# A graph network kernel: a third x1 buffer, own buffers for the ninth slot, transposed sums, and the diagonal taken off TensorE

## The chip, the cores and the metric

The kernel runs on one NeuronCore of a Trainium2 chip. Its time is the device time in microseconds of one execution; the figure compared is the median of several executions. The engines are TensorE (PE for its matmuls and PEld for its weight loads in the profile), VectorE (DVE), ScalarE (ACT) and GpSimd (POOL). Each works through its own queue in order, so an instruction that waits holds back all that stand behind it on its engine. DMA transfers are issued from the queue of SyncE (SP).

## The reference

There are 32 independent batch elements, each a graph of N = 512 nodes with D = 128 features. The adjacency matrix has about one entry in sixteen set, and a full diagonal.

```python
# layer 0
a = adj + eye(N); d = a.sum(axis=2) ** -0.5          # 0 where the degree is 0
x = layernorm(x + (d[:, :, None] * a * d[:, None, :]) @ (x @ w0) + b0)
# layer 1
m_j, m_i = x @ W1[:D], x @ W1[D:]
pre = m_j[:, None, :, :] + m_i[:, :, None, :] + b1     # [B, i, j, D]
msg = gelu(layernorm(pre) * g1 + be1)                  # exact gelu
agg = einsum('bijo,bij->bio', msg, adj)
upd = layernorm(concat([x, agg]) @ W2 + b2) * g2 + be2
out = layernorm(x + upd)
```

The costly part is layer 1: a layer norm and a gelu for each edge (i, j).

## The kernel before

The nodes of an element are cut into C = 4 chunks of P = 128. An adjacency matrix is thus 4 x 4 blocks (q, c). For each row of each block the kernel lists its edges, works through them one edge per row at a time, and leaves zeros of the matrix alone.

**Slots.** Eight *list slots* hold the eight first edges of each row in each block. A small *ninth slot* (`EXTRA`) holds one more edge per row of the four diagonal blocks. Two *shared slots* hold what is left over, packed. The list slots and the shared slots take four turns each (one for each q), the ninth slot one, so an element takes 8 x 4 + 1 + 2 x 4 = 41 turns of the main loop. In the ninth slot `gathered` loads a vector of 516 numbers to all partitions and `gathers` compares it with the partition's number (`s`, 128 x 516); in the other slots both have 2052 numbers. `gathers` also starts a transposing DMA of `s` into `mt`.

**One turn.** `pairs` (TensorE) gathers, by one-hot matmuls, the pre-activation of 512 edges into a PSUM tile `u` (three buffers). One turn later `sums` (DVE, L733) adds the part of the node itself and writes `u_sb`, and `weights` (POOL, L748) makes `sw`, the one-hot matrix times the adjacency values. Two turns later `messages` (ACT, L762) writes the gelu `m` in four activations. Three turns later `aggregate` (TensorE, L771) adds `sw` times `m` into the PSUM tile `agg`. The shared slots skip `sums`; there ACT reads `u` itself. `raw` of a slot is loaded five turns ahead of it, and its `s` is made three turns ahead.

**Work beside the turns.** The other steps are generators that are advanced a few steps per turn. `prepare` runs a plan of six of them, each given a stretch of turns: `layer0` (26 steps) from turn 41 before its element begins to turn 19 before, then `lists`, `parts`, `factors`, `more` and `shared`. Counted in the turns of element b, `layer0(b+2)` occupies turns 41 to 62. After the last `aggregate` of an element, at turn 43, `finish(b)` is appended to `todo` and advanced one step per turn, ahead of the plan's steps of that turn. `finish` transposes `agg`, multiplies by W2, adds the bias, normalises (L194 and L196 on DVE, L199 to L205 on POOL, L208 on ACT), applies g2 and be2 and adds x1 (L642, L644, L646, on POOL), normalises again and stores the result.

For the turns from 43 on this gives, on the engines of the change:

- ACT, turn 43: copy of agg (L780), m, and layer 0's copies; turn 44: m, `aggt` (L629) and copies; turn 47: m, four counts (L291), four scaled copies that make `s` (L295); turn 49: m, the activation `un`; turn 52: m(50), the activation that writes `x1` of element b+2; then m(51), m(52) and, at turn 55, the activation `o_sb`.
- DVE, turn 51: u_sb(50), `y` (L311) and its statistics; turn 52: u_sb(51) and steps of `shared`; turn 53: u_sb(52), the statistics of `un`.
- POOL, turn 50 to 52: one of L642, L644 and L646 each, behind that turn's `sw`; the small steps of y's layer norm stand in turn 51, those of `un`'s in turn 54.

The order of ACT, POOL and DVE is the order in which the program is written (`manual_schedule`). The order on TensorE and SP is chosen by the framework, which also places the semaphores: a tile with `bufs=n` has n buffers for its tag, and a write into a buffer waits until the readers of the tile that held it before are done.

In layer 0 the diagonal of `adj + eye` is not added to the matrix: the node's own part is one more matmul, of the identity with `s` (L306), into the same PSUM sum.

Of the kernel before, what the change touches and what calls it, by code (L numbers as in the profile page):

```python
# [8 lines left out]
F32 = mybir.dt.float32  # L9
BF16 = mybir.dt.bfloat16  # L10
I32 = mybir.dt.int32
U32 = mybir.dt.uint32
AF = mybir.ActivationFunctionType
ALU = mybir.AluOpType
# [4 lines left out]
P = 128  # L19
# [4 lines left out]
PAD = 4  # L24
# [3 lines left out]
def bcast(ap, n):  # L28

    return ap.unsqueeze(1).to_broadcast([ap.shape[0], n, ap.shape[-1]])  # L30
# [16 lines left out]
def sparse_path(ctx, tc, x, adj, w0, b0, w1, b1, g1, be1, w2, b2, g2, be2, out, most):  # L47
# [21 lines left out]
    nc = tc.nc  # L69
    B, N, D = x.shape  # L70
    C = N // P
# [3 lines left out]
    node = ctx.enter_context(tc.tile_pool(name="node", bufs=1))  # L75
    small = ctx.enter_context(tc.tile_pool(name="small", bufs=2))
    onehot = ctx.enter_context(tc.tile_pool(name="onehot", bufs=2))
# [3 lines left out]
    ps_g = ctx.enter_context(tc.tile_pool(name="ps_g", bufs=1, space=PSUM))  # L81
# [3 lines left out]
    ident = const.tile([P, P], F32, name="ident")  # L85
# [45 lines left out]
    node_p = const.tile([P, 1], F32, name="node_p")  # L131
# [12 lines left out]
    for name, src in (("b0", b0), ("b1", b1), ("g1", g1), ("be1", be1), ("b2", b2), ("g2", g2), ("be2", be2)):  # L144
        t = const.tile([P, D], F32, name=f"{name}_row")
# [34 lines left out]
    for k in range(n_sd):  # L180
        t = const.tile([P, C, C, P], BF16, name=f"sd_rows{k}")
# [31 lines left out]
    def bank(key):  # L213
        return ps.tile([P, 512], F32, tag="ps", name=key)

    def transposed(src, key):

        pt = bank(f"pt_{key}")
        for c in range(C):
            nc.tensor.transpose(pt[:, c * P : (c + 1) * P], src[:, c, :], ident)  # L220
        return pt
# [3 lines left out]
    def pause(n):  # L225

        for _ in range(n):
            yield

    def layer0(b):  # L230

        st = state[b] = {}
# [6 lines left out]
        a_t = big.tile([P, C, C, WIDE], F32, tag="a_t", name=f"a_t_{b}", bufs=2)  # L239
# [6 lines left out]
        for mc in range(C):  # L246
            pt = bank(f"pa_{b}_{mc}")
# [4 lines left out]
            if mc == 2:  # L252
                psup = bank(f"psup_{b}")
# [29 lines left out]
        rsqrt(rdeg, degp)  # L283
        dinv = small.tile([P, C], F32, tag="dinv", name=f"dinv_{b}")
        nc.gpsimd.tensor_sub(dinv, rdeg, none)
        xb = node.tile([P, C, D], F32, tag="t2", name=f"xb_{b}")
        nc.gpsimd.tensor_tensor(xb, xs, bcast(rows["b0"], C), ALU.add)

# [4 lines left out]
        s = node.tile([P, C, D], F32, tag="t1", name=f"s_{b}")  # L293
        for c in range(C):
            nc.scalar.activation(  # L295
                s[:, c, :], psup[:, c * P : (c + 1) * P], AF.Copy, scale=dinv[:, c : c + 1]
            )
        yield from pause(2)
        pt = bank(f"pconv_{b}")
        for c in range(C):  # L300
            o = pt[:, c * P : (c + 1) * P]
            for mc in range(C):
                nc.tensor.matmul(
                    o, a_t[:, mc, c, :P], s[:, mc, :], start=(mc == 0), stop=False
                )
            nc.tensor.matmul(o, ident, s[:, c, :], start=False, stop=True)  # L306
            if c % 2:
                yield
        y = node.tile([P, C, D], F32, tag="t3", name=f"y_{b}")
        for c in range(C):  # L310
            nc.vector.scalar_tensor_tensor(  # L311
                y[:, c, :], pt[:, c * P : (c + 1) * P], dinv[:, c : c + 1], xb[:, c, :], ALU.mult, ALU.add
            )
        x1 = node.tile([P, C, D], F32, tag="x1", name=f"x1_{b}", bufs=2)
        yield from layernorm(y, x1, f"l0_{b}")
        st["x1"] = x1
        yield
        pt = transposed(x1, f"x1_{b}")
# [32 lines left out]
        for q in range(C + 1):  # L351
# [4 lines left out]
            if q < C:  # L356
                pt = bank(f"pv_{b}_{q}")
# [96 lines left out]
    def shared(b):  # L454

        st = state[b]
# [22 lines left out]
        pt = bank(f"po_{b}")  # L479
# [32 lines left out]
        pt = None  # L512
        for k in range(len(chunks) + 1):
            if k:
                nc.vector.tensor_scalar(sj_f[:, chunks[k - 1]], pt, node_p, None, ALU.is_equal)  # L515
            if k < len(chunks):
                pt = bank(f"pj_{b}_{k}")
# [6 lines left out]
        for n in range(C * C + 1):  # L524
            if n:
                nc.scalar.copy(sent[:, n - 1], pt[:, : SHARED * WIDE].rearrange("p (k w) -> p k w", w=WIDE))  # L526
            if n < C * C:
                pt = bank(f"pl_{b}_{n}")
                for k in range(SHARED):
# [4 lines left out]
                        start=True,  # L534
                        stop=True,
# [28 lines left out]
        n_i = SHARED * C + 1  # L564
        pt = bank(f"pidx_s_{b}")
# [5 lines left out]
        nc.gpsimd.tensor_scalar(ve[:, :n_r], picked[:, 1, :], 0.0, None, ALU.max)  # L571
        nc.gpsimd.tensor_scalar(ve[:, n_r:], var[:, own, 0], 0.0, None, ALU.max)
        yield
        idx_r = node.tile([n_i, N], BF16, tag="idx_rs", name=f"idx_rs_{b}")
        nc.scalar.copy(idx_r, pt[:n_i, :])
        sd = small.tile([P, n_r + C], F32, tag="sd_s", name=f"sd_s_{b}", bufs=1)
        nc.scalar.activation(sd, ve, AF.Sqrt, bias=eps_t, scale=1.0 / D)
# [6 lines left out]
        pt = bank(f"psd_s_{b}")  # L584
# [38 lines left out]
    def finish(b):  # L623

        st = state.pop(b)
        pt = transposed(st["agg_sb"], f"g_{b}")
        yield
        aggt = node.tile([P, N], F32, tag="f1", name=f"aggt_{b}")
        nc.scalar.copy(aggt, pt)  # L629
        yield  # L630
        pt = bank(f"pu_{b}")
        for c in range(C):
            o, here = pt[:, c * P : (c + 1) * P], slice(c * P, (c + 1) * P)
            nc.tensor.matmul(o, st["x1t"][:, here], w2_sb[:, 0, :], start=True, stop=False)
            nc.tensor.matmul(o, aggt[:, here], w2_sb[:, 1, :], start=False, stop=True)
        yield
        u = node.tile([P, C, D], F32, tag="f0", name=f"u_{b}")
        nc.vector.tensor_tensor(u, pt.rearrange("p (c d) -> p c d", d=D), bcast(rows["b2"], C), ALU.add)
        yield
        un = node.tile([P, C, D], F32, tag="f1", name=f"un_{b}")  # L640
        yield from layernorm(u, un, f"l1_{b}")
        nc.gpsimd.tensor_tensor(un, un, bcast(rows["g2"], C), ALU.mult)  # L642
        yield
        nc.gpsimd.tensor_tensor(un, un, bcast(rows["be2"], C), ALU.add)  # L644
        yield
        nc.gpsimd.tensor_tensor(un, un, st["x1"], ALU.add)  # L646
        yield
        o_sb = node.tile([P, C, D], F32, tag="o_sb", name=f"o_sb_{b}")
        yield from layernorm(un, o_sb, f"l2_{b}")
        yield  # L650
        nc.sync.dma_start(out[b].rearrange("(c p) d -> p c d", p=P), o_sb)
# [4 lines left out]
    EXTRA = SLOTS  # L656
# [5 lines left out]

    def gathered(b, t):

        raw = onehot.tile([P, 3, (C * N + PAD) // 3 + 2], BF16, tag="raw", name=f"raw_{b}_{t}", bufs=1)
        if t < SLOTS:
            src, n0, n = state[b]["idx_d"], t * C, C
        elif t == EXTRA:
            src, n0, n = state[b]["idx_ds"], SHARED * C, 1
        else:  # L670
            src, n0, n = state[b]["idx_ds"], (t - EXTRA - 1) * C, C
        n = n * N + PAD
        s = raw[:, :, : n // 3]
        nc.sync.dma_start(
            s, src[n0 * N : n0 * N + n].partition_broadcast(P).rearrange("p (k e) -> p k e", k=3)
        )
        return s

    def gathers(b, t, raw):


        n = 1 if t == EXTRA else C
        s = onehot.tile([P, C * N + PAD], BF16, tag="s1", name=f"s1_{b}_{t}")
        nc.vector.tensor_scalar(  # L684
            s[:, : n * N + PAD].rearrange("p (k e) -> p k e", k=3), raw, node_p, None, ALU.is_equal
        )
        mt = onehot.tile([P, C, C, P], BF16, tag="mt", name=f"mt_{b}_{t}", bufs=3)
        nc.sync.dma_start_transpose(out=mt[:, :n].rearrange("p c q i -> p (c q) i"), in_=s[:, : n * N])
        made_s[b, t] = s[:, : C * N].rearrange("p (c j) -> p c j", j=N)
        return mt  # L690

    def deviations(b, t):
# [72 lines left out]
    def aggregate(b, t, q, m, sw):  # L765
        st = state[b]
        begin, end = (t, q) == order[0], (t, q) == order[-1]
        if begin:
            st["agg"] = ps_g.tile([P, C, D], F32, tag="agg", name=f"agg_{b}")
        for c in range(C):  # L770
            nc.tensor.matmul(  # L771
                st["agg"][:, c, :],
                sw[:, c, :],
                m[:, c, :],
                start=(begin and c == 0),
                stop=(end and c == C - 1),
            )
        if end:
            st["agg_sb"] = node.tile([P, C, D], F32, tag="f0", name=f"agg_sb_{b}")
            nc.scalar.copy(st["agg_sb"], st["agg"])  # L780
            todo.append(finish(b))

    def advance(gens, steps=1):
# [9 lines left out]
    made_r, made_s, made_m, made_d = {}, {}, {}, {}  # L793
# [3 lines left out]
    n_groups = len(order)  # L797
    plan = [
        (layer0, 26, -n_groups, -19),
        (lists, 21, -19, -8),  # L800
        (parts, 7, -19, -10),
        (factors, 7, -8, -3),
        (more, 33, -10, 8),
        (shared, 45, 8, 28),
    ]
    running = {}
# [21 lines left out]
    def fetch(g):  # L828

        if g + 5 in begins:  # L830
            made_r[begins[g + 5]] = gathered(*begins[g + 5])
        if g + 3 in begins:
            here = begins[g + 3]
            made_m[here] = gathers(*here, made_r[here])
            made_d[here] = deviations(*here)
# [6 lines left out]
    def pass_on():  # L842

        if active:
            aggregate(*active.pop(0))
        ready = summed.pop(0) if summed else None
        if gathered_c:
            key, pu = gathered_c.pop(0)
            summed.append((key, sums(*key, pu), weights(*key)))
        if ready:  # L850
            key, u, sw = ready
            active.append((*key, messages(*key, u), sw))
# [292 lines left out]
```

## Time and profile before

| | |
|---|---|
| median of 3 runs | 4140.36 us (4138.46 to 4145.49) |
| the profiled execution | 4133.86 us |
| its span, first to last instruction | 4131.9 us |
| mean granted TensorE clock | 0.967 |
| PE, PEld busy | 3860.8 us (93%), 3603.1 us (87%) |
| DVE, ACT, POOL busy | 3241.0 us (78%), 2777.9 us (67%), 2178.9 us (53%) |
| L771, matmuls of `agg` | 10496, busy 1507.3 us |
| L723, L724, matmuls of `u` | 20992, busy 1452.5 and 1160.9 us |

A line of the timeline gives the start and the length in microseconds, the engine, the line of the kernel, the operation and its tiles, the shape, how many instructions are merged, and in brackets the idle time of the engine before it with what ended it. A line of the waits gives who waited for whom, the total in microseconds, how often, and the longest. A line of the windows gives a stretch, its length, for each engine in the order PE, PEld, DVE, ACT, POOL its busy time, then the granted clock as a share of full speed, the DMA share and GB/s. An f32 product of 128 x 128 x 128 is two matmul instructions.

### The profile page before, as it was taken

What the parts mean: (1) busy time and instruction counts of PE and PEld (TensorE: products, weight loads), DVE (VectorE), ACT (ScalarE), POOL (GpSimd) and SP (SyncE); (2) the same over time, 40 slices, a digit from 0 to 9 for tenths busy, and PEclk for the clock granted to TensorE, in tenths of its full rate; (3) what the DMA queues carried; (4) which work ended last, traced back from release to release, by engine and by line L of the source; (5) the groups of instructions that cost most, each with busy time, mean ns of one, the idle gap of its engine ahead of it and who ended that gap; (6) DMA issues with size and microseconds to landing.
All of it is one profiled execution on the core that took longest, in us unless ns stands there. A gap on an engine that the chain in (4) does not pass through costs nothing. (4 is left out here: it accounts for less than half of the span.)

```text
span 4131.9 us, 108903 instructions
## 1 busy us (share of the span) xinstructions
PE 3860.8 (93%) x40128; PEld 3603.1 (87%) x40128; DVE 3241.0 (78%) x10645; ACT 2777.9 (67%) x8225; POOL 2178.9 (53%) x2462
## 2 busy tenths in 40 slices
PE   6999999999999999999999999999999999999997
PEld 5988889888898888898888988889988889888887
DVE  6777787777887788877778877888777788778882
ACT  4666676666676766766666667666666676676664
POOL 4455564555655555545555455555455564555544
PEclk8999999999999999999999999999999999999998
DMA  3444444444444444444444444444444544444442
GB/s 85 110 99 101 113 96 103 102 100 106 101 105 106 98 104 110 98 109 104 100 107 96 103 110 96 105 113 93 112 99 101 113 96 103 109 97 104 101 101 57
DMA packets 902107, 420.01 MB, mean 102 GB/s; under 512 B 724304, under 2 KB 882192, under 8 KB 901568
## 3 DMA queue, kind: packets, MB, share of 16 engines
q1 hardware_dynamic: 901344, 412.52, 43.3%
q8 instruction: 320, 5.24, 0.5%
q14 instruction: 219, 1.79, 0.1%
q0 software_dynamic: 224, 0.46, 0.1%
HBM read 227.15 MB, written 13.76 MB: 58 GB/s over the span
## 5 line engine op out<-in xcount | busy, mean ns | idle before, releaser
L748 POOL TENSOR_TENSOR sw<-mt,a_t 128x512 f32<-128x512 bf16 x1056 | 1219.4, 1165 | 985.0 <-PE agg L771 929.1
L771 PE MATMUL agg<-m,sw 128*128 128x128 f32 x10496 | 1507.3, 287 | 119.6 <-ACT m L762 119.6
L723 PE MATMUL u<-c,s 128*128 128x128 bf16 x15744 | 1452.5, 223 | 85.3 <-DVE u_sb L733 81.8
L771 PEld LDWEIGHTS agg<-m,sw 128*128 128x128 f32 x10496 | 1320.5, 195 | 132.7 <-POOL a_t L495 123.2
L762 ACT ACTIVATE m<-u_sb,r 128x128 f32<-128x128 f32 x4096 | 1294.9, 393 | 172.7 <-DVE u_sb L733 100.2
L723 PEld LDWEIGHTS <-s 128*128 128x128 bf16 x15744 | 1214.4, 100 | 170.9 <-DVE u_sb L733 68.9
L724 PE MATMUL u<-be,sd_rows 128*128 128x128 bf16 x5248 | 1160.9, 222 | 5.2 <-DMA sd_rows<-sd_d 4.1
L733 DVE TENSOR_TENSOR u_sb<-u,ac 128x512 f32<-128x512 f32 x1056 | 713.5, 676 | 199.3 <-PE u L724 179.7
L724 PEld LDWEIGHTS <-sd_rows 128*128 128x128 bf16 x5248 | 521.1, 100 | 12.9 <-issue 4.8
L684 DVE TENSOR_SCALAR s<-raw,node_p 128x2052 bf16<-128x2052 bf16 (+1 forms) x352 | 421.3, 1197 | 101.9 <-DMA raw<-idx_ds 58.2
L748 POOL TENSOR_TENSOR sw<-mt,sent 128x512 f32<-128x512 bf16 x256 | 297.2, 1164 | 296.1 <-PE agg L771 229.6
L762 ACT ACTIVATE m<-u,r_s 128x128 f32<-128x128 f32 x1024 | 288.5, 363 | 236.5 <-PE agg L771 231.8
L719 PE MATMUL u<-ac,sj 128*128 128x128 f32 x2048 | 444.1, 299 | 0.0
L526 ACT COPY sent<-pl 128x352 f32<-128x352 f32 x512 | 229.0, 448 | 314.6 <-PE pl L530 278.0
L530 PEld LDWEIGHTS pl<-a_t,sj 128*128 128x128 f32 x2048 | 316.7, 191 | 63.4 <-issue 59.3
L530 PE MATMUL pl<-a_t,sj 128*128 128x176 f32 x2048 | 328.2, 313 | 4.0 <-POOL a_t L498 4.0
L450 DVE MAX8 a_t<-key 128x8 f32<-128x128 f32 x1024 | 301.1, 294 | 34.5
L719 PEld LDWEIGHTS u<-ac,sj 128*128 128x128 f32 x2048 | 314.2, 194 | 0.3
L515 DVE TENSOR_SCALAR sj<-pj,node_p 128x512 f32<-128x512 f32 x256 | 187.6, 745 | 139.6 <-PE pj L519 139.6
L451 DVE FIND_INDEX8 idx_m<-a_t,key 128x8 uint32<-128x128 f32 x1024 | 291.3, 285 | 0.0
L354 DVE SCALAR_TENSOR_TENSOR key<-pv,a_sum,c_sum 128x512 f32<-128x512 f32 x128 | 95.6, 748 | 108.4 <-PE pv L358 108.4
L208 ACT ACTIVATE x<-y,shift_l,rstd_l 128x128 f32<-128x128 f32 x128 | 52.7, 481 | 150.2 <-POOL un L646 137.5
(180 smaller groups left out, 4904.4 us busy)
## 6 DMA issues: line engine op xcount, KB each, us to landing
raw<-idx_d SPq DMA_DIRECT2D x256, 513.0 KB
raw<-idx_ds SPq DMA_DIRECT2D x64, 513.0 KB
a_nat<-in_adj_dram SPq DMA_DIRECT2D x32, 1024.0 KB
sd_rows<-sd_d SPq DMA_DIRECT2D x768, 12.0 KB
xs<-in_x_dram SPq DMA_DIRECT2D x32, 256.0 KB
out_dram<-o_sb SPq DMA_DIRECT2D x32, 256.0 KB
mt<-s SPq DMA_TRANSPOSE x352
raw<-idx_ds SPq DMA_DIRECT2D x32, 129.0 KB
```

Of the source, the lines that this page charges most:

```text
L450: nc.vector.max(found, k)
L451: nc.vector.max_index(idx[:, n, h : h + 8], found, k)
L526: nc.scalar.copy(sent[:, n - 1], pt[:, : SHARED * WIDE].rearrange("p (k w) -> p k w", w=WIDE))
L530: nc.tensor.matmul(pt[:, k * WIDE : (k + 1) * WIDE], sj[:, n, k * P : (k + 1) * P], at[:, n, :], start=True, stop=True,)
L684: nc.vector.tensor_scalar(s[:, : n * N + PAD].rearrange("p (k e) -> p k e", k=3), raw, node_p, None, ALU.is_equal)
L719: nc.tensor.matmul(pu[:, c, :], place, state[b]["ac"][:, q, 0, :], start=first, stop=False)
L723: nc.tensor.matmul(pu[:, c, :], here, c3[:, k, c, :], start=(first and k == 0), stop=False)
L724: nc.tensor.matmul(pu[:, c, :], dev[:, q, c, :], be9, start=False, stop=(c == C - 1))
L733: nc.vector.tensor_tensor(u, pu, a if t == EXTRA else bcast(a[:, q, :], C), ALU.add)
L748: nc.gpsimd.tensor_tensor(sw, mt[:, 0] if t == EXTRA else mt[:, :, q, :], a, ALU.mult)
L762: nc.scalar.activation(m[:, c, :], u[:, c, :], AF.Gelu, scale=r[:, k : k + 1])
L771: nc.tensor.matmul(st["agg"][:, c, :], sw[:, c, :], m[:, c, :], start=(begin and c == 0), stop=(end and c == C - 1),)
```

## The change

Five things are changed.

1. `x1` has three buffers instead of two.
2. The ninth slot has storage of its own for `raw` (one buffer) and for `s` (one buffer); the others keep one buffer of `raw` and two of `s`.
3. In `aggregate`, `sw` and `m` trade places as stationary and moving operand, so that the sum over j comes out with features on partitions. `finish` then needs no transposes of it, and is two steps shorter: the one copy out of PSUM is already `aggt`.
4. In layer 0 the identity's matmul is left out. ACT scales the PSUM tile `psup` a second time, by the square of `dinv`, into `own_s`, and POOL adds that to `xb` (the input plus the bias). The square is one more small POOL instruction.
5. Some storage is shared: `idx_rs` uses that of `idx_r`, `o_sb` that of `u` (tag `f0`), `own_s` that of `y` (tag `t3`).

```diff
@@ layer0
         nc.gpsimd.tensor_sub(dinv, rdeg, none)
+        dinv2 = small.tile([P, C], F32, tag="dinv2", name=f"dinv2_{b}", bufs=1)
+        nc.gpsimd.tensor_tensor(dinv2, dinv, dinv, ALU.mult)
...
+        own_s = node.tile([P, C, D], F32, tag="t3", name=f"own_s_{b}")
+        for c in range(C):
+            nc.scalar.activation(
+                own_s[:, c, :], psup[:, c * P : (c + 1) * P], AF.Copy, scale=dinv2[:, c : c + 1]
+            )
         yield from pause(2)
+        nc.gpsimd.tensor_tensor(xb, xb, own_s, ALU.add)
...
                 nc.tensor.matmul(
-                    o, a_t[:, mc, c, :P], s[:, mc, :], start=(mc == 0), stop=False
+                    o, a_t[:, mc, c, :P], s[:, mc, :], start=(mc == 0), stop=(mc == C - 1)
                 )
-            nc.tensor.matmul(o, ident, s[:, c, :], start=False, stop=True)
...
-        x1 = node.tile([P, C, D], F32, tag="x1", name=f"x1_{b}", bufs=2)
+        x1 = node.tile([P, C, D], F32, tag="x1", name=f"x1_{b}", bufs=3)
@@ shared
-        idx_r = node.tile([n_i, N], BF16, tag="idx_rs", name=f"idx_rs_{b}")
+        idx_r = node.tile([n_i, N], BF16, tag="idx_r", name=f"idx_rs_{b}")
@@ finish
-        pt = transposed(st["agg_sb"], f"g_{b}")
-        yield
-        aggt = node.tile([P, N], F32, tag="f1", name=f"aggt_{b}")
-        nc.scalar.copy(aggt, pt)
-        yield
+        aggt = st["aggt"]
...
-        o_sb = node.tile([P, C, D], F32, tag="o_sb", name=f"o_sb_{b}")
+        o_sb = node.tile([P, C, D], F32, tag="f0", name=f"o_sb_{b}")
@@ gathered
-        raw = onehot.tile([P, 3, (C * N + PAD) // 3 + 2], BF16, tag="raw", name=f"raw_{b}_{t}", bufs=1)
...
         n = n * N + PAD
+        raw = onehot.tile([P, 3, n // 3 + 2], BF16, tag=f"raw{n}", name=f"raw_{b}_{t}", bufs=1)
@@ gathers
-        s = onehot.tile([P, C * N + PAD], BF16, tag="s1", name=f"s1_{b}_{t}")
...
+        s = onehot.tile([P, n * N + PAD], BF16, tag=f"s{n}", name=f"s_{b}_{t}", bufs=1 if t == EXTRA else 2)
...
@@ aggregate
-            st["agg"] = ps_g.tile([P, C, D], F32, tag="agg", name=f"agg_{b}")
+            st["agg"] = ps_g.tile([P, C, P], F32, tag="agg", name=f"agg_{b}")
...
+                m[:, c, :],
                 sw[:, c, :],
-                m[:, c, :],
...
-            st["agg_sb"] = node.tile([P, C, D], F32, tag="f0", name=f"agg_sb_{b}")
-            nc.scalar.copy(st["agg_sb"], st["agg"])
+            st["aggt"] = node.tile([P, N], F32, tag="f1", name=f"aggt_{b}")
+            nc.scalar.copy(st["aggt"], st["agg"].rearrange("p c i -> p (c i)"))
```

More of the change, by code (lines that the diff above doesn't have):

```diff
@@ L682, in gathers @@
         n = 1 if t == EXTRA else C
-        s = onehot.tile([P, C * N + PAD], BF16, tag="s1", name=f"s1_{b}_{t}")
-        nc.vector.tensor_scalar(
-            s[:, : n * N + PAD].rearrange("p (k e) -> p k e", k=3), raw, node_p, None, ALU.is_equal
-        )
+        s = onehot.tile([P, n * N + PAD], BF16, tag=f"s{n}", name=f"s_{b}_{t}", bufs=1 if t == EXTRA else 2)
+        nc.vector.tensor_scalar(s.rearrange("p (k e) -> p k e", k=3), raw, node_p, None, ALU.is_equal)
         mt = onehot.tile([P, C, C, P], BF16, tag="mt", name=f"mt_{b}_{t}", bufs=3)
         nc.sync.dma_start_transpose(out=mt[:, :n].rearrange("p c q i -> p (c q) i"), in_=s[:, : n * N])
-        made_s[b, t] = s[:, : C * N].rearrange("p (c j) -> p c j", j=N)
+        made_s[b, t] = s[:, : n * N].rearrange("p (c j) -> p c j", j=N)
         return mt
```

## The prediction

> **What bounds the kernel now.** I read the page first, then the waits, then the timeline of one batch element (the seventeenth, 2002.66 to 2129.01 us), then windows over its two gaps. Turn n is pass n of the main loop, 41 to an element; m(n), sw(n), u_sb(n) and agg(n) are the pieces of turn n's pairs.
>
> ```profile
> PE 3860.8 (93%) x40128; PEld 3603.1 (87%) x40128; DVE 3241.0 (78%) x10645; ACT 2777.9 (67%) x8225; POOL 2178.9 (53%) x2462
> ...
> ACT x L208 <- POOL un L646: 137.5, 30, 4.6
> PE agg L771 <- ACT m L762: 119.6, 31, 4.0
> PE u L723 <- DVE u_sb L733: 81.8, 68, 3.3
> DVE s L684 <- DMA raw<-idx_ds: 58.2, 21, 4.5
> DVE s L684 <- PE agg L771: 39.3, 15, 2.9
> ```
>
> TensorE is the bound, but it stands still twice per element. The gaps recur every 126.35 us (2129.01 - 2002.66). Gap 1 is about 3.96 us, gap 2 about 1.84 us in most elements.
>
> ```profile
> 2121.07 1.28 ACT L762 ACTIVATE m<-u_sb,r 128x128 f32<-128x128 f32 x4
> 2126.93 1.65 ACT L208 ACTIVATE x<-y,shift_l,rstd_l 128x128 f32<-128x128 f32 x4 [4.58 <-POOL un L646]
> 2128.48 2.44 ACT L762 ACTIVATE m<-u_sb,r 128x128 f32<-128x128 f32 x8
> ...
> 2124.31 0.24 POOL L205 TENSOR_SCALAR shift_l<-shift_l 128x4 f32<-128x4 f32 x1
> 2124.51 1.16 POOL L748 TENSOR_TENSOR sw<-mt,a_t 128x512 f32<-128x512 bf16 x1
> 2125.63 1.26 POOL L646 TENSOR_TENSOR un<-un,x 128x512 f32<-128x512 f32 x1
> ...
> 2128.98 1.11 PEld L771 LDWEIGHTS agg<-m,sw 128*128 128x128 f32 x8 [4.10 <-POOL a_t L495]
> ...
> 2129.01 1.27 PE L771 MATMUL agg<-m,sw 128*128 128x128 f32 x8 [3.95 <-ACT m L762]
> ```
>
> Gap 1: x1 of element b+2 needs the buffer that `finish(b)` still reads on POOL (L646). ACT stands in front of it for 4.58 us with m(51) queued behind, and agg(51) starts 0.14 us after m(51)'s first quarter. ACT could not have gone at once: shift, its other input, ended at 2124.55.
>
> ```profile
> 2060.18 1.28 DVE L684 TENSOR_SCALAR s<-raw,node_p 128x2052 bf16<-128x2052 bf16 x1 [2.42 <-PE agg L771]
> ...
> 2062.11 0.50 PE L723 MATMUL u<-c,s 128*128 128x128 bf16 x3 [1.79 <-DVE u_sb L733]
> ...
> 2060.00:2062.00 2.00, 0.33 (x4) 0.15 (x3) 1.82 (x3) 0.00 (x0) 2.00 (x2) 0.98 0.07 17
> 2062.00:2064.00 2.00, 1.89 (x16) 1.58 (x17) 1.90 (x10) 1.31 (x5) 1.28 (x2) 0.50 0.69 132
> ...
> 2130.00:2132.00 2.00, 2.00 (x14) 1.66 (x14) 2.00 (x4) 0.94 (x5) 1.83 (x4) 0.54 0.00 0
> ```
>
> Gap 2: s of the first shared slot waits for a `raw` whose load could start only after the ninth slot's small s had read the single buffer (2055.49 to 2055.97), and for the s buffer of slot 7. The seventh number of a window is the granted clock: 0.50 behind either gap.
>
> **Clock.** Going through the clock over all elements, every gap 1 is followed by 3.4 or 6.8 us at 0.50, costing about 1.9 us of work; some 15 of 31 gaps 2 are, so 1.0 us on average. Gaps and clock together are 3.96 + 1.9 + 1.84 + 1.0 = 8.7 us an element.
> The Trainium skill (TensorE: Matmul & The Clock Gate, The HAM clock gate) lets the clock fall after an idle window of about 3.4 us; the gaps of 1.84 us here halve it about half the time, so the trace disagrees. By the page, short gaps left over would be free and the sum below would be about 20 us lower.
>
> **Ninth slot's buffers.** `raw` and s of the small slot get their own storage, so the load starts at turn 28 with its buffer free since turn 25, and s at turn 30 finds a buffer free since slot 6. DVE would start that s at about 2057.7, after L393, and u_sb(29) at 2058.9; TensorE wants it at 2060.3. Gap 2 goes: 1.84 + 1.0 = 2.8 us. Behind it lie slots whose m is ready 4 to 7 us before use, so TensorE keeps the gain. Bounds: 1.0 (half the gap stays) to 2.84; I take 2.8.
>
> **Work taken from TensorE.** L306: 4 products an element, each 0.22 us (2112.82 to the next start 2113.04): 0.9. The transposes in `finish`: 0.5 (2096.30 to 2096.80). Both lie between the copy of agg (ACT, 2095.66) and gap 1, whose end is set by other engines. So 0 of 1.4 us, unless gap 1 goes entirely.
>
> **Features on partitions.** The two operands of L771 trade places, same shape and type. m now feeds the weight load: its bounds are 0 and one 0.19 us load (mean 195 ns) for each group that finds m just made, at most 41 x 0.19 = 7.8 us an element. Matched one by one, only 4.7 of 41 groups start within 0.25 us of their m. And the line above shows that load at 2128.98 although its sw had ended at 2125.67: it already waits behind m. I take 0.
> The Trainium skill (same page, What happens when you issue a matmul) says weight loads are pulled ahead of matmuls; by that this swap would expose 4.7 x 0.19 = 0.9 us an element, 28 in all. The 2128.98 row speaks against it.
>
> **ACT and POOL.** Added per element: own_s, 4 activations like L295 (2110.45 to 2111.45), 1.0 us; on POOL dinv2, 0.2 like L285, and one 1.27 like L287. Gone: the aggt copy, 0.47 of ACT (2100.06 to 2100.53). `finish` is two steps shorter, so its activation of un (1.54) moves from turn 49 to 47, its three POOL adds to turns 48, 49, 50, its last bn_stats before y's at turn 51, its shift to turn 52. ACT is full from 2095.66 to 2112.7, so m(46) comes at 2111.45 + 1.54 + 1.0 - 0.47 = 2113.5; TensorE waits there some 2 us. It pays for that with the 1.4 us it was relieved of, and reaches agg(51) at about 2125.3 against 2124.95. The new add gives y's input one more writer: own_s ends by 2113.5, POOL then adds to about 2116, and y is due at 2120.4, with u_sb(51) queued behind it; the bank of psup is held 1.0 us longer. If this cover fails, own_s and its adds cost up to 2.5 us an element (77 in all).
>
> **x1 with three buffers: what is late next.** DVE is busy from 2106.3 to 2125.0. bn_stats of u (1.1) leaves this stretch and that of un (1.15) enters it ahead of y, so y's statistics end at 2122.6 against 2122.5. POOL's four small steps then make shift at 2124.65; ACT does x1 to 2126.3, then m(51), and agg(51) starts at 2126.7. Next POOL does sw(51), the steps of un's norm (2.0, formerly turn 54), the five of L492 to L498 (2.1), sw(52): 2124.65 + 1.15 + 2.0 + 2.2 + 1.15 = 2131.15. agg(52), at 2133.05 now, waits for that. TensorE then runs agg(52), two pj and the next pairs, 0.95 + 0.43 + 0.89 (start to start at full clock), so agg(53) starts at 2133.4 instead of 2135.58 (timeline): 2.2 saved at full clock, 0.9 if the new waits (1.4 and 1.85) again halve it. Gap 2 says even odds or worse for a single wait: 1.5. Bounds: -0.5 (the clock falls for 6.8 us) to 3.96 + 1.9 = 5.9.
>
> **Free changes.** idx_rs in idx_r's storage: written 6 turns apart. o_sb in f0: leaves at turn 55, next u a full element later. Bound for both: 0 to 0.3 us.
>
> **Sum.** 31 x (2.8 + 1.5) = 133; the tail loses a transpose and a copy, 1.5. The profiled execution took 4133.86 (span 4131.9 and 2.0 around it), so 3999; the median of 4140.36 lies 6.5 above it: 4005.
>
> **Rivals.**
> Both gaps vanish (0.17): shift and sw come earlier than I drew them. For: POOL idles 2.31 us before y's shift. Against: it idles for DVE, which is full. 8.7 + 1.4 = 10.1 an element: 4140 - 313 = 3827.
> x1 buys nothing (0.20): sw(52) takes the place of L646, with the clock halved for 6.8 us. For: POOL is busy 1.83 of the 2 us shown from 2130. Against: it stood idle 2.31 us just before y's shift, and TensorE has work until 2125.3. 4140 - 31 x 2.8 = 4053, or down to 4085 if gap 2 leaves a rest.
> Exposed weight loads (0.04): 4033.
> Slower (0.08): the pile on ACT at turn 47 (m, un, four counts, s, own_s). m(46) has 0.14 us of margin today. TensorE waits 2.1 us and the clock falls (1.9): 4.0, and if late pconv holds up y (slack 1.6 us), gap 1 stays whole. It decides once that loss exceeds gap 2's 2.8: 31 x (4.0 - 2.8) = 37, so 4177. Against: 1.4 us of TensorE's work went from this very stretch.
> No effect (0.04): the waits keep their length under other names; 4140.
>
> **How the numbers follow.** The forecast of 4005 has 0.47, its own range 3950 to 4045 from the bounds of 1.5. Differences under 0.2% (8 us) can't be told from none. Faster is 0.47 + 0.17 + 0.20 + 0.04 = 0.88, same 0.04, slower 0.08. The range 3860 to 4115 leaves out the last two and half of the first rival.
>
> **What would show it.** Right: ACT x loses its wait for POOL un and waits for shift about 2 us; DVE s's waits vanish; TensorE's gap near turn 30 is under 0.5 us, gap 1 splits into two of 1 to 2 us, the second ending with sw. Wrong: a gap over 2.5 us before pconv or agg(46); L771's groups slower than 0.95 us; agg(53) following y's statistics by much more or less than 10.8 us.

## The result and the profile after

The changed kernel takes 4012.69 us (median of 4 runs, 4008.96 to 4014.48) against 4141.6 us of the kernel before on the same chip (4138.46 to 4145.49): a ratio of 0.9687, interval 0.967 to 0.9704. It is faster; the forecast was 4005. Its profiled execution took 4011.64 us.

The page of the changed kernel, the span, the engines' busy times and one group of instructions (lines moved by the edit: L771 is now L772, L762 is L763, L684 is L687, L733 is L734, L748 is L749):

```profile
span 4009.9 us, 108439 instructions
...
PE 3766.3 (94%) x39744; PEld 3510.3 (88%) x39744; DVE 3263.9 (81%) x10645; ACT 2791.9 (70%) x8321; POOL 2225.5 (55%) x2526
...
L687 DVE TENSOR_SCALAR s<-raw,node_p 128x2052 bf16<-128x2052 bf16 (+1 forms) x352 | 421.5, 1197 | 20.6 <-DMA raw<-idx_ds 11.9
```

TensorE's busy time fell by 94.5 us (3860.8 to 3766.3), of which the clock is a part: over the whole trace the time lost to the halved clock (half of the time spent at 0.50) fell from 138.4 to 59.2 us. TensorE's idle time between its first and its last matmul fell only from 244.6 to 217.2 us. DVE's idle time before s (L687) fell from 101.9 to 20.6 us: that wait was the cause of gap 2.

The waits (who waited for whom, total in us, times, longest):

```profile
ACT x L208 <- POOL shift_l L205: 104.2, 32, 7.8
...
PE u L724 <- DVE u_sb L734: 80.3, 69, 2.2
...
PEld pconv L311 <- ACT s L297: 55.4, 31, 6.7
...
PE agg L772 <- POOL sw L749: 46.1, 30, 1.6
...
PE agg L772 <- ACT m L763: 30.0, 20, 1.5
...
DVE s L687 <- DMA raw<-idx_ds: 11.9, 13, 4.1
```

x1's activation has lost its wait for L646 and waits for its shift. TensorE waits for m 20 times, at most 1.5 us, instead of 31 times at 4 us. It waits 30 times for `sw` and 69 times for `u_sb` (before, 68 times, mostly at gap 2; now in front of gap 1's old place), and its weight load before `pconv` waits for layer 0's `s`, which ACT makes.

One element (the sixteenth) on the timeline, ACT, then POOL, then TensorE:

```profile
1937.24 1.65 ACT L208 ACTIVATE x<-y,shift_l,rstd_l 128x128 f32<-128x128 f32 x4 [3.04 <-POOL shift_l L205]
1938.80 1.26 ACT L763 ACTIVATE m<-u_sb,r 128x128 f32<-128x128 f32 x4
```
```profile
1936.97 0.24 POOL L205 TENSOR_SCALAR shift_l<-shift_l 128x4 f32<-128x4 f32 x1
1937.17 1.17 POOL L749 TENSOR_TENSOR sw<-mt,a_t 128x512 f32<-128x512 bf16 x1
1938.42 0.23 POOL L199 TENSOR_SCALAR ve_l<-mv_l 128x4 f32<-128x4 f32 x1
...
1942.47 4.53 POOL L749 TENSOR_TENSOR sw<-mt,a_t 128x512 f32<-128x512 bf16 x4
```
```profile
1921.97 0.33 PE L724 MATMUL u<-c,s 128*128 128x128 bf16 x3 [0.84 <-DVE u_sb L734]
...
1924.52 0.27 PE L724 MATMUL u<-c,s 128*128 128x128 bf16 x1 [1.50 <-DVE u_sb L734]
1924.53 0.50 PEld L311 LDWEIGHTS pconv<-s,a_t 128*128 128x128 f32 x2 [1.62 <-ACT s L297]
...
1939.33 1.27 PE L772 MATMUL agg<-sw,m 128*128 128x128 f32 x8
...
1943.69 1.16 PE L772 MATMUL agg<-sw,m 128*128 128x128 f32 x8 [1.54 <-POOL sw L749]
```

shift ends at 1937.21, x1 starts at 1937.24, m(51) at 1938.80, agg(51) at 1939.33. The norm of `un` stands in front of `sw(52)` on POOL (1938.42), so the first of the four `sw` merged at 1942.47 ends at about 1943.6, and agg(52) starts at 1943.69. This is the chain that the prediction drew. The wait that ends at 1924.52 has two causes at once: `u_sb` ended at 1924.47 and so did the first half of the four activations that make `s`.

In this element the clock had fallen (see the windows below), and TensorE came to agg(51) only about 0.1 us ahead of its m. In the 19 of 30 elements of the loop in which the clock stayed full, TensorE is there earlier and waits, as in this one:

```profile
2674.35 1.27 PE L772 MATMUL agg<-sw,m 128*128 128x128 f32 x8 [1.52 <-ACT m L763]
2678.70 1.16 PE L772 MATMUL agg<-sw,m 128*128 128x128 f32 x8 [1.53 <-POOL sw L749]
```

These are the two gaps into which gap 1 was to split.

Gap 2's place on DVE in the sixteenth element:

```profile
1992.22 0.48 DVE L687 TENSOR_SCALAR s<-raw,node_p 128x516 bf16<-128x516 bf16 x1
...
1994.41 1.26 DVE L687 TENSOR_SCALAR s<-raw,node_p 128x2052 bf16<-128x2052 bf16 x1
```

s of the first shared slot starts with no idle time in front of it, and TensorE with none at this place.

Two windows that hold new waits, and the one behind (the clock is the last number but two):

```profile
1924.00:1926.00 2.00, 1.48 (x8) 1.41 (x8) 1.93 (x8) 2.00 (x9) 2.00 (x3) 0.52 0.47 147
...
1942.00:1944.00 2.00, 0.46 (x5) 0.32 (x3) 1.81 (x5) 2.00 (x8) 2.00 (x3) 1.00 1.01 191
1944.00:1946.00 2.00, 2.00 (x26) 1.75 (x25) 0.90 (x2) 2.00 (x7) 2.00 (x3) 1.00 1.09 249
```

The clock is at 0.52 behind the waits that end at 1921.97 and 1924.52, and at 1.00 behind the wait for sw(52). Of the 30 elements of the loop 11 have a stretch at 0.50, each time behind this first pair of waits and never behind those at agg(51) and agg(52); before, every element had at least one.

To compare runs I took, from each trace, the median over 26 elements (from the copy of the third to that of the twenty-eighth) of a few starts, counted from the copy of `agg` to SBUF at turn 43, and the mean length of an element in these:

| us from the copy of agg | y | x1 | agg(51) | agg(52) | agg(53) | product of x1t | agg(59) | element |
|---|---|---|---|---|---|---|---|---|
| before | 24.67 | 31.26 | 33.34 | 37.60 | 39.92 | 40.87 | 68.68 | 126.70 |
| changed | 25.33 | 29.55 | 31.64 | 35.99 | 38.31 | 39.26 | 67.07 | 122.65 |
| p_x1 | 24.66 | 28.91 | 30.99 | 34.53 | 37.15 | 39.83 | 67.75 | 125.92 |
| p_ninth | 24.66 | 31.25 | 33.33 | 37.86 | 40.21 | 41.16 | 68.97 | 124.64 |
| p_sums | 25.06 | 29.30 | 31.38 | 35.75 | 38.07 | 39.02 | 66.83 | 124.87 |
| p_own | 25.30 | 31.89 | 33.98 | 38.22 | 40.49 | 41.43 | 69.24 | 127.31 |
| a_ident | 25.06 | 29.29 | 31.38 | 35.74 | 38.06 | 39.00 | 66.82 | 122.88 |
| a_later | 24.80 | 29.04 | 31.12 | 34.67 | 37.29 | 39.96 | 67.88 | 123.45 |
| a_norm | 25.32 | 29.63 | 31.71 | 34.37 | 38.14 | 39.39 | 67.30 | 122.59 |
| a_pu | 26.56 | 30.80 | 32.88 | 37.26 | 39.59 | 40.53 | 68.35 | 124.14 |
| a_both | 23.14 | 28.66 | 30.74 | 33.96 | 37.17 | 38.40 | 66.32 | 121.97 |
| a_last | 23.13 | 28.68 | 30.76 | 33.43 | 35.70 | 36.65 | 65.29 | 121.18 |

The trace of p_own is that of its slowest execution (4156.6 us against a median of 4140.34), so its element reads about 0.5 us too long.

An element is 4.05 us shorter. By the means over the same elements, 1.87 of that lies in the stretch of gap 1 (to agg(59), 69.00 to 67.13; the medians of the table differ by 1.61) and 2.18 in the rest, where gap 2 was (57.70 to 55.52). In the stretch of gap 1 TensorE's idle time did not fall: it rose from 4.43 to 4.97 us an element. What fell there is the cost of the halved clock, from 2.49 to 0.59; the remaining 0.5 is less work. In the rest, idle time fell from 2.05 to 0.67 and the cost of the clock from 0.98 to nothing.

### The profile page after: what moved, and what is told of

Same layout as the page of the kernel before. It is cut to its first block, busy times and chain, and to the rows that moved or that the text cites. A ratio compares the mean times of both kernels' runs of the same rounds, so it can differ in the third digit from the quotient of the medians.

```text
span 4009.9 us, 108439 instructions
## 1 busy us (share of the span) xinstructions
PE 3766.3 (94%) x39744; PEld 3510.3 (88%) x39744; DVE 3263.9 (81%) x10645; ACT 2791.9 (70%) x8321; POOL 2225.5 (55%) x2526
## 5 line engine op out<-in xcount | busy, mean ns | idle before, releaser
L749 POOL TENSOR_TENSOR sw<-mt,a_t 128x512 f32<-128x512 bf16 x1056 | 1216.8, 1164 | 918.1 <-PE agg L772 764.0
L772 PE MATMUL agg<-sw,m 128*128 128x128 f32 x10496 | 1495.7, 285 | 76.2 <-POOL sw L749 46.1
L724 PE MATMUL u<-c,s 128*128 128x128 bf16 x15744 | 1433.9, 220 | 84.0 <-DVE u_sb L734 80.3
L763 ACT ACTIVATE m<-u_sb,r 128x128 f32<-128x128 f32 x4096 | 1294.0, 395 | 142.3 <-DVE u_sb L734 57.8
L772 PEld LDWEIGHTS agg<-sw,m 128*128 128x128 f32 x10496 | 1304.5, 192 | 94.2 <-POOL sw L749 51.3
L724 PEld LDWEIGHTS <-s 128*128 128x128 bf16 x15744 | 1191.2, 98 | 115.0 <-issue 40.9
L725 PE MATMUL u<-be,sd_rows 128*128 128x128 bf16 x5248 | 1148.6, 220 | 20.7 <-DMA sd_rows<-sd_ds 14.6
L734 DVE TENSOR_TENSOR u_sb<-u,ac 128x512 f32<-128x512 f32 x1056 | 713.4, 676 | 200.6 <-PE u L725 177.1
L725 PEld LDWEIGHTS <-sd_rows 128*128 128x128 bf16 x5248 | 512.7, 98 | 30.7 <-issue 20.0
L763 ACT ACTIVATE m<-u,r_s 128x128 f32<-128x128 f32 x1024 | 288.3, 363 | 251.6 <-PE agg L772 247.4
L687 DVE TENSOR_SCALAR s<-raw,node_p 128x2052 bf16<-128x2052 bf16 (+1 forms) x352 | 421.5, 1197 | 20.6 <-DMA raw<-idx_ds 11.9
L749 POOL TENSOR_TENSOR sw<-mt,sent 128x512 f32<-128x512 bf16 x256 | 296.4, 1163 | 229.0 <-PE agg L772 176.2
L537 PEld LDWEIGHTS pl<-a_t,sj 128*128 128x128 f32 x2048 | 316.2, 191 | 60.7 <-issue 59.2
L311 PEld LDWEIGHTS pconv<-s,a_t 128*128 128x128 f32 x1024 | 141.3, 214 | 57.1 <-ACT s L297 55.4
```

Of the source, the lines that this page charges most:

```text
L537: nc.tensor.matmul(pt[:, k * WIDE : (k + 1) * WIDE], sj[:, n, k * P : (k + 1) * P], at[:, n, :], start=True, stop=True,)
L687: nc.vector.tensor_scalar(s.rearrange("p (k e) -> p k e", k=3), raw, node_p, None, ALU.is_equal)
L724: nc.tensor.matmul(pu[:, c, :], here, c3[:, k, c, :], start=(first and k == 0), stop=False)
L725: nc.tensor.matmul(pu[:, c, :], dev[:, q, c, :], be9, start=False, stop=(c == C - 1))
L734: nc.vector.tensor_tensor(u, pu, a if t == EXTRA else bcast(a[:, q, :], C), ALU.add)
L749: nc.gpsimd.tensor_tensor(sw, mt[:, 0] if t == EXTRA else mt[:, :, q, :], a, ALU.mult)
```

## Experiments

Theories: (1) the two waits and what is late behind them set the time; (2) the products taken from TensorE do. Each run stands beside runs of the kernel before on its chip.

### One part at a time on the kernel before

**The third x1 buffer alone (p_x1).**

```diff
-        x1 = node.tile([P, C, D], F32, tag="x1", name=f"x1_{b}", bufs=2)
+        x1 = node.tile([P, C, D], F32, tag="x1", name=f"x1_{b}", bufs=3)
-        idx_r = node.tile([n_i, N], BF16, tag="idx_rs", name=f"idx_rs_{b}")
+        idx_r = node.tile([n_i, N], BF16, tag="idx_r", name=f"idx_rs_{b}")
```

> The kernel before with nothing but the third x1 buffer (and idx_rs in idx_r's storage, to make room). Theory (the two gaps): x1's activation no longer waits for L646, it waits for its shift (2124.55 in the element shown), so agg(51) starts at 2126.7 instead of 2129.0. L646 and the norm of un keep their old turns, so sw(52) ends at 2130.1 as before, earlier than in the full change (2131.2), and agg(53) starts at about 2132.4 instead of 2135.6: 1.9 to 3.2 us an element, 4040 to 4085 us, likeliest 4065. Rival (the work taken from TensorE is what pays): nothing is taken here, so 4141 as before. Rival (the wait only changes its name): under 1 us an element, over 4110.

Measured: 4111.12 us against 4137.57, ratio 0.9937 (0.992 to 0.9953): 26 us, under half of the least I expected, and what the second rival had (over 4110). Its waits:

```profile
ACT x L208 <- POOL shift_l L205: 80.3, 32, 10.8
...
PE pat L326 <- ACT x1t L321: 47.8, 31, 1.6
...
PE agg L771 <- POOL sw L748: 21.6, 30, 0.7
```

The x1 wait changed as foreseen, and agg(51), agg(52) and agg(53) came 2.35, 3.07 and 2.77 us earlier. What I had not seen is the second line: the product that reads x1t now waits for its copy on ACT (31 times, 1.6 us), and only 1.04 us of the gain is left at it (40.87 to 39.83), 0.93 at agg(59).

```profile
1988.07 1.65 ACT L208 ACTIVATE x<-y,shift_l,rstd_l 128x128 f32<-128x128 f32 x4 [2.23 <-POOL shift_l L205]
...
1996.83 1.65 ACT L208 ACTIVATE o_sb<-un,shift_l,rstd_l 128x128 f32<-128x128 f32 x4
1998.38 0.56 ACT L321 COPY x1t<-pt_x 128x512 f32<-128x512 f32 x1
```

The copy (L321) stands behind `o_sb` on ACT, and `o_sb` waits for the norm of `un`, which in this kernel still stands at turns 53 to 55.

A part of the gain is lost again later. By the means the stretch to agg(59) is 1.29 us shorter (69.00 to 67.71) and the rest 0.52 longer: gap 2 is still there, and it now halves the clock in 21 of the 26 elements instead of 12. In the stretch itself TensorE idles as long as before (4.47 us against 4.43), but in waits of about 1.6, 0.7 and 1.6 us instead of one of 3.96, and the clock falls behind them in none of the 30 elements.

**The ninth slot's buffers alone (p_ninth).** The edit is the diff's `gathered` and `gathers`, with idx_rs in idx_r's storage.

> The kernel before with nothing but the ninth slot's own raw and s (and idx_rs in idx_r's storage). Theory: gap 2 goes with its clock, 1.84 + 1.0 = 2.8 us an element: 4055 us, 4045 to 4075; gap 1 stays at 3.96 us. Rival (DVE is full there and falls behind anyway): half of it, about 4100. Rival (work): 4141.

Measured: 4071.27 us, ratio 0.9845 (0.9827 to 0.9863): 66 us, or 2.06 an element, in the expected range.

```profile
ACT x L208 <- POOL un L646: 137.3, 30, 4.6
...
PE u L722 <- DMA sd_rows<-sd_ds: 17.2, 27, 3.7
PE pidx L401 <- ACT idx_h L397: 17.1, 20, 5.1
...
DVE s L684 <- DMA raw<-idx_ds: 13.5, 19, 3.4
```

The waits of s are nearly gone (13.5 us for `raw` and 1.1 for the buffer of s are left of 58.2 and 39.3), gap 1 is there with the x1 wait unchanged at 137.3. Per element 1.96 us of idle time went and 0.92 us of halved clock; waits of 0.34 us for `sd_rows` and 0.29 us for `idx_h`, just behind, took part of it back. `raw` and s got their storage in one run, so what each of the two is worth is not shown.

**The transposed sums alone (p_sums).** The edit is the diff's `finish` and `aggregate`, with o_sb in f0; x1 keeps two buffers.

> The kernel before with nothing but the transposed sums and the finish that is two steps shorter (o_sb in f0); x1 has two buffers. Theory: finish now reads x1 (POOL, L646) at turn 50, two turns ahead of the write of the next x1 at turn 52, so the x1 wait goes without a third buffer, and sw(52) at about 2131 is the next one late: gap 1 shrinks as in the full change, 0.9 to 2.2 us an element, about 4095 us (4070 to 4115). Rival (only the transposes' 0.5 us count): 4125. Rival (weight loads of m exposed, 0.9 us an element): slower than that by 28.

Measured: 4083.3 us, ratio 0.9872 (0.9855 to 0.9888): 54 us, in the expected range.

```profile
PE u L719 <- DVE u_sb L729: 145.8, 103, 3.0
...
ACT x L208 <- POOL shift_l L205: 107.4, 32, 9.8
...
DVE s L680 <- DMA raw<-idx_ds: 63.4, 22, 4.0
...
PE agg L767 <- POOL sw L744: 46.7, 31, 1.6
```

The x1 wait for L646 is gone with two buffers: the shorter `finish` alone removes it. The new waits for `u_sb` and for `sw` are those of the changed kernel. Gap 2's waits are still there.

**The node's own part alone (p_own).** The edit is the diff's `layer0` without the third buffer.

> The kernel before with nothing but the node's own part outside TensorE (dinv2, own_s, one POOL add; no identity product). Theory: the 0.9 us it takes from TensorE stand in front of gap 1 and are absorbed; ACT's 1.0 us more stands before m(46), which has 0.14 us to spare: no gain, 4135 to 4175 us, likeliest 4150. Rival (work taken from TensorE pays): 32 x 0.9 = 28 less, 4113.

Measured: 4140.34 us, ratio 1.0008 (0.9998 to 1.0018): nothing that can be told.

```profile
ACT x L208 <- POOL un L653: 137.4, 30, 4.6
PE agg L778 <- ACT m L769: 137.1, 33, 4.5
```

TensorE has 0.9 us less to do an element and waits longer for m: 4.5 us each time, against 4.0. y starts 0.63 us later.

The three parts that gain make 26 + 66 + 54 = 146 us; the whole change made 129. The third buffer and the shorter `finish` remove the same wait, and without the third buffer the sum is 120 (the change without it, a_x1two below, makes 124).

### One part undone in the changed kernel

**Two x1 buffers (a_x1two)**: `bufs=3` back to `bufs=2`.

> The changed kernel with two x1 buffers again. Theory: since finish is two steps shorter, L646 ends some 6 us before x1's activation starts (1930.8 and 1937.2 in the element looked at), so the third buffer does nothing: 4013 us within 6. Rival (the third buffer is what removed the x1 wait): gap 1 comes back, 1.5 us an element or more, 4059 or over.

Measured: 4014.77 us, ratio 0.9708 (0.9692 to 0.9724), against 0.9687 of the change. Every start of the table is the same within 0.01 us. The third buffer does nothing here:

```profile
ACT x L208 <- POOL shift_l L205: 106.1, 32, 8.9
```

**The operands of L772 in their old places (a_roles).**

```diff
-                m[:, c, :],
                 sw[:, c, :],
+                m[:, c, :],
```

> The changed kernel with sw and m in their old places in L771's product (sw stationary, m moving), all else as in the change; what is added up is then the sum over j with nodes on partitions, and the rest of finish takes it as if transposed. Theory: the weight load stood behind m before as after, so nothing moves: 4013 us within 6. Rival (the page's pulled-ahead weight loads): the old places are better by 0.9 us an element, 3985.

Measured: 4013.02 us, ratio 0.9704 (0.9688 to 0.9721); every start is the same. (This kernel leaves out the transposition that `finish` would then need, so its output is not the layer's; its instructions and their shapes are those of the change.) Which operand is stationary made no difference.

The trace says why. In the kernel before, in the changed one and in this one, a wait for the semaphore of m, a separate instruction of TensorE's queue, ends just ahead of the first weight load of agg(51) in 30 of 31 elements: before, it ends at 2128.95 and the load starts at 2128.98. The program holds the load until m is there, whichever operand it loads.

**`finish` in its old turns (a_later).**

```diff
         aggt = st["aggt"]
+        yield from pause(2)
```

> The changed kernel with two idle steps at the head of finish, so that its steps stand in the turns they had before. Theory: un's activation leaves ACT's pile at turn 47 and un's norm leaves POOL's queue ahead of sw(52); with three x1 buffers L646 at turn 52 holds nothing back. The gaps of 0.84 and 1.50 us near turn 47 shrink and sw(52) ends 1.0 us earlier: 1 to 2.5 us an element, 3935 to 3980 us, likeliest 3960. Rival (the early finish is what pays): slower, 4030 or over.

Measured: 4032.52 us, ratio 0.9747 (0.973 to 0.9763): 20 us slower than the change, so the rival was right. As in p_x1, agg(53) comes earlier (37.29 against 38.31) and the product of x1t later (39.96 against 39.26):

```profile
PE agg L773 <- ACT m L764: 67.0, 33, 2.1
...
PE pat L333 <- ACT x1t L328: 43.4, 31, 1.6
```

**The identity product back (a_ident).** dinv2, own_s and the POOL add are taken out, L306 is put back.

> The changed kernel with the identity product back in TensorE and own_s, dinv2 and the POOL add gone. Theory: the 0.9 us lies ahead of gap 1 and is absorbed, while ACT's pile at turn 47 and POOL lose 1.0 and 1.5 us: the same or faster, 3985 to 4015 us, likeliest 4000. Rival (TensorE's work pays): 28 slower, 4041.

Measured: 4023.62 us, ratio 0.9725 (0.9709 to 0.9742): 11 us slower than the change, and 9 to 11 slower than a_x1two and a_roles on the same chip. The theory (the same or faster) was wrong, and the rival was too large.

The clock shows where the loss lies. In the 16 of 30 elements in which it stays full, the stretch to agg(59) is even 0.26 us shorter with the product in TensorE (66.81 against 67.07 us), and TensorE waits 0.57 us for m in front of agg(51), against 1.52 in the change: the difference is about the 0.9 us of work. In the other 14 the clock falls behind the waits of 0.84 and 1.50 us, for 3.4 us as a rule, which takes about 1.7 us of work. That is more than the 0.57 us to spare, so agg(51) comes 1.0 us later (32.39 against 31.37) and the stretch takes 67.83 us. In the change, with 1.52 us to spare, the 11 elements with a halved stretch take 67.23. So the work taken from TensorE pays where the clock falls. Over 30 elements this makes 0.16 us each, and the rest of an element 0.06; the few us that are left of the 11 are not settled.

### Toward a better order

In the changed kernel DVE stands still for the products of `finish`, which it now wants one turn after the copy:

```profile
1907.49 0.67 DVE L734 TENSOR_TENSOR u_sb<-u,ac 128x512 f32<-128x512 f32 x1
1910.20 0.69 DVE L641 TENSOR_TENSOR u<-pu,b_row 128x512 f32<-128x512 f32 x1 [2.03 <-PE pu L638]
```

**`finish`'s last norm one turn later (a_norm).**

```diff
+        yield
         yield from layernorm(un, o_sb, f"l2_{b}")
```

> The changed kernel with one idle step in finish ahead of its last layer norm, so that un's statistics stand at turn 52 instead of 51 (behind y's on DVE), its POOL steps at turn 53 (behind sw(52)), o_sb at turn 54. Theory: the wait left over is agg(52) for sw(52), 1.54 us an element; sw(52) ends 2.0 us earlier and y's statistics 1.2 earlier, so 1.2 to 2 us an element go: 3950 to 3975 us. Rival (what the run with the third buffer alone showed: x1t's copy stands behind o_sb on ACT and becomes late): under 0.5 us an element, 3998 or over.

Measured: 4015.02 us, ratio 0.97 (0.9684 to 0.9716): no gain, as the rival had it, though by another instruction. The wait for sw(52) went (agg(52) 1.62 us earlier), but `o_sb` now stands on ACT before its shift is made, with m(53) behind it, and agg(53) gains 0.17. The clock also fell in more elements (1.12 us lost an element, against 0.59):

```profile
ACT o_sb L208 <- POOL shift_l L205: 98.6, 32, 17.9
```

**u's add one turn after its products (a_pu).**

```diff
-        yield
+        yield from pause(2)
         u = node.tile([P, C, D], F32, tag="f0", name=f"u_{b}")
...
         nc.gpsimd.tensor_tensor(un, un, bcast(rows["g2"], C), ALU.mult)
-        yield
         nc.gpsimd.tensor_tensor(un, un, bcast(rows["be2"], C), ALU.add)
```

> The changed kernel with u's DVE add one turn later than its products (turn 45 instead of 44), and the adds of g2 and be2 in one turn, so that L649 stays at turn 50. Theory: DVE no longer waits 2.0 us for the products and un's activation leaves the pile on ACT at turn 47, so the waits of 0.84 and 1.50 us for u_sb go; but the end of the stretch is set by DVE and ACT, so only 0.4 to 1.5 us an element are kept: 3965 to 4000 us, likeliest 3990. Rival (TensorE's gaps are worth what they measure): 2.3 us an element, 3940.

Measured: 4053.31 us, ratio 0.9798 (0.9781 to 0.9814): 41 us slower, where theory and rival both had a gain. DVE's wait for the products went, and another took its place: POOL comes to L649's add later (it is L648 here), and the statistics of `un`, ahead of y on DVE, wait for it, so y starts 1.23 us later. The halved clock costs 2.82 us an element here, against 0.59.

```profile
1954.70 0.87 DVE L194 BATCH_NORM_STATS2 stats_l<-un 128x6 f32<-128x128 f32 x4 [3.67 <-POOL un L648]
```

**Both (a_both).**

> Both of these edits together. Theory: they act on different waits and add up: 1.6 to 3.5 us an element, 3905 to 3965 us, likeliest 3940. Rival (one chain, no sum): no better than the better of the two.

Measured: 3992.65 us, ratio 0.9647 (0.9631 to 0.9663): 20 us faster than the change, less than expected, but neither edit gains anything alone. With the statistics of `un` behind y, DVE keeps what it won, and y starts 2.19 us earlier.

**The last norm three turns later (a_last)**: a_both with `yield from pause(3)` in place of the one yield ahead of the last norm.

> Both edits of the run before (3992.65 us), with three idle steps instead of one ahead of finish's last layer norm: un's statistics at turn 54, o_sb at turn 56, behind x1t's copy (turn 55). Theory: with the one idle step x1t's copy ends 0.05 us before the product that reads it, behind o_sb and the wait for its shift; with three it is free, and so is m(53): 0.3 to 0.7 us an element better, 3965 to 3985 us. Rival (the stretch ends with m(51), behind y's statistics, whatever stands after it): 3993 within 6.

Measured: 3968.95 us (3968.67 to 3972.56), ratio 0.959 (0.9572 to 0.9607): 44 us faster than the change, the best of all and in the expected range. x1t's copy now stands ahead of `o_sb` on ACT, and its product comes 1.75 us earlier than with one idle step. What TensorE still waits for:

```profile
PE agg L772 <- ACT m L763: 64.7, 32, 2.1
...
PE u L724 <- DVE u_sb L734: 24.4, 40, 1.6
...
PE agg L772 <- POOL sw L749: 8.8, 31, 0.3
```

agg(51) for m is 2.1 us an element; m(51) stands behind x1's activation, and that behind y and its norm. In this kernel y is held by a part of the change itself: DVE waits for the POOL add of `own_s` to `xb` (L306), which stands behind two of `un`'s steps on POOL.

```profile
DVE y L318 <- POOL xb L306: 32.8, 25, 1.3
```

In the changed kernel no such wait is seen. What it would bring to move this add, or to put the identity's product back here, was not tried.

## Why the prediction was right

**Gap 1.** Expected 1.5 us an element, measured 1.61 by the medians (68.68 to 67.07) and 1.87 by the means. The chain held: counted from the copy of agg, agg(51) was put at 31.0 and came at 31.6, the end of sw(52) at 35.5 and came at 35.9, agg(53) at 37.7 at full clock and came at 38.3. From the end of y's statistics to agg(53) it took 11.0 us, where 10.8 were drawn.

That the size fits so well is in part luck. The 1.5 stood between 2.2 us at full clock and 0.9 with the clock halved behind the new waits. The clock stayed full there, so the figure that applied was 2.2. What brought it down to 1.6 is that the chain began late: y's statistics were to end 0.1 us later than before and ended 0.63 later (27.27 against 26.64 after the copy of agg). The start of y moved by 0.39 us with the shorter `finish` alone (p_sums), and by 0.27 more with the own part (25.33 against 25.06 in a_ident).

What the prediction got wrong is the cause: the wait went because `finish` is shorter (p_sums, a_x1two), not because x1 has a third buffer. The third buffer alone removes the same wait, but gains less (p_x1), and beside the shorter `finish` nothing (a_x1two). The prediction itself put L646 at turn 50, which is enough to see it.

**Gap 2.** Expected 2.8 us, measured 2.18 in the whole change (means of the rest of an element) and 2.06 alone. The wait itself (1.96 us an element) went entirely, and the clock's cost with it (0.98, where 1.0 was put); the term was too large because small waits for `sd_rows` and `idx_h` stood right behind. The two terms erred in opposite directions: 4.3 us were expected and 4.05 measured.

**The clock.** Over the loop the halved clock's cost fell from 3.48 to 0.59 us an element, in the stretch of gap 1 from 2.49 to 0.59. TensorE's idle time fell by less than one would think from the gaps: two waits of 0.84 and 1.50 us came in near turn 47. The prediction had TensorE wait some 2 us there, for m(46) behind the pile on ACT. It is `u_sb` that it waits for, and in the second wait `s` of that pile as well, which ends at the same moment. The prediction left out that DVE would wait for the products of `finish` at turn 44 (2.03 us at 1910.20). For TensorE these waits lay ahead of agg(51) and cost little, as the prediction had it for its own wait: 0.16 us in the 11 elements in which the clock fell behind them.
The Trainium skill (TensorE: Matmul & The Clock Gate, The HAM clock gate) has the clock fall after an idle window of about 3.4 us. In the changed kernel the longest recurring idle time is 1.55 us, and 11 elements still show a halved stretch, behind two waits of 2.3 us together: shorter waits sufficed here, so the trace disagrees.

**The swap** was put at 0 and measured at 0 (a_roles). The rule that weight loads are pulled ahead (the Trainium skill, same page, What happens when you issue a matmul) would, by the prediction's estimate, have made the old places better by 28 us. The runs do not bear that out (4013.02 against 4012.69 us), nor do they test the rule: the program's own wait for m stands ahead of the load.

**Work taken from TensorE** was put at 0 of 1.4 us. Alone the own part made nothing (p_own); within the change it is worth 9 to 11 us, about 0.3 an element (a_ident), by the margin that it leaves where the clock falls. The term was too small by that.

**Rivals.** Both gaps vanishing (3827) and x1 buying nothing (4053) did not come as times, though a_x1two shows that the third buffer itself buys nothing beside the shorter `finish`. The pile on ACT came as waits but did not decide.

## What to carry to other kernels

When an in-order queue waits at an instruction, write down what else that instruction needs and when each engine behind it would be ready: that gave this result within 0.2%, helped by two errors that cancelled in part, while taking each wait at its full size gave 3827 us, 186 too few. A buffer and an earlier reader can remove the same wait, so try each alone before paying memory. In an order that is written out by hand, try shifts in pairs too: here two that gain nothing alone gained 20 us together, and 44 with the norm moved behind the copy that the next products need.

## What the runs showed of the hardware

In the kernel before, the gaps of 3.96 us were followed by a stretch at half clock in all 30 elements of the loop, those at gap 2 (1.6 to 3.2 us) in 14 of them. Shorter waits did so or not, in pairs that differ in how close they stood (no run varied the distance alone). In the changed kernel the waits of 0.84 and 1.50 us, with 1.05 us between them (1921.97 to 1923.02), halved the clock in 11 of 30 elements; the waits of 1.52 and 1.53 us at agg(51) and agg(52), with 2.8 us between them (2674.35 to 2677.17), in none of the 19 elements that have both, and those of 1.6, 0.7 and 1.6 us in p_x1 in none of 30. Breaking up the gap of 4 us therefore won by the clock and not by idle time: in p_x1 the idle time of the stretch stayed (4.43 and 4.47 us an element), and the cost of the halved clock went from 2.49 us to nothing.

What a halved stretch cost depended on the time to spare behind it: ahead of agg(51) it took 0.16 us where TensorE otherwise waited 1.52 us (the change), and 1.0 us where it otherwise waited 0.57 (a_ident).

In the kernel before, an f32 product whose stationary `sw` had been ready for 3.3 us (2125.67 to 2128.98) loaded its weights only once the moving operand was there, behind a wait that the program puts in front of the load. With such a wait, making the late operand the stationary one cost nothing (a_roles).
